# Quartered divisions in two self attentions, the last experts' answers as rows, and answers fetched in two parts

## The chip, the core and the metric

The kernel runs on one core of a Trainium2 chip. A core has a matrix engine (TensorE, "PE" in the profile, its weight loads "PEld"), a vector engine (VectorE, "DVE"), a scalar engine (ScalarE, "ACT"), a general engine (GpSimd, "POOL") and a queue engine (SyncE, "SP"), which only issues transfers here. They run side by side, each through its own list of instructions in order, and wait for one another by semaphores. The metric is the device time of one execution in microseconds (us); lower is better.

## What is computed

A two-layer perceiver with 512 latent rows of width 512, 16 heads of 32, and a context of 8192 rows. Each layer is a cross attention into the context, a self attention, and a mixture of eight experts of which every row takes two. Everything is float32.

```python
x = x + L0_xattn(layernorm(x), ctx, key_mask, ...)      # LayerNorm on the heads of q and k
x = x + L0_attn(layernorm(x), ...)                      # softmax over j >= i
x = x + L0_ffn(layernorm(x), router, W1, W2)            # 8 experts, hidden width 2048, SiLU
x = x + L1_xattn(layernorm(x), ctx, mask, ...)
x = x + L1_attn(layernorm(x), ...)                      # 64 neighbours of each row
x = x + L1_ffn(layernorm(x), Wg, W1, W2)                # 8 experts, hidden width 1024, relu squared

def L1_ffn(x, Wg, W1, W2):
    probs = softmax(x @ Wg)
    top_w, top_i = top_k(probs, 2)
    top_w = top_w / (sum(top_w) + 1e-8)
    combine = sum(one_hot(top_i, 8) * top_w[..., None], axis=1)
    h = square(relu(einsum('td,edh->teh', x, W1)))
    y = einsum('teh,ehd->ted', h, W2)
    return einsum('te,ted->td', combine, y)
```

Which rows go to which expert depends on the data. The inputs are drawn from a fixed seed.

## The kernel before

The whole program is unrolled, and a scheduler orders each engine's list: an instruction that is ready in its model goes ahead of one that is not, and ties go by program order. So the order of the trace is that of the program with some instructions moved forward into holes. In time the stages are: cross attention 0 (0 to 467 us), self attention 0 (to 626), experts 0 (to 925), cross attention 1 (to 1333), self attention 1 (to 1443), experts 1 (to 1658), end (to 1667.9).

**Cross attentions** (`attend_slots`). The context is reduced to 15 tiles of 128 keys. Heads go in four groups `g` of four. For each group and tile a step computes scores (L787), subtracts the maximum (L668), takes the exponential (L914), and multiplies with the values (L864); the maxima of later groups are taken in the same steps, so that the last group's steps have none. When a group's 15 steps are over, its closing work is put as "fillers" behind the next group's steps: the sum of the exponentials (L894) at step 2, the division in quarters (`divide`, L906) at steps 3 to 6, then a multiplication and a bias on POOL (L909, L911), and the product with the output matrix (`k.outputs`, L744) at steps 9 and 10, followed by additions to the residual `x` on DVE (L750).

**Self attentions.** `in_order` goes through a string written by hand: `q`, `k` projections, `M` maxima, `S` the three parts of finding the shift of a group, `W` exponentials and sums, `F` the end of a group, `O` the output product in two halves. `F` copies the sum `o` and the denominator `d` out of PSUM on ACT, then does one reciprocal of 128x512 on DVE (L711), one multiplication on DVE (L712) and, in layer 0, a bias on ACT (L715). `S` needs DVE as well: a reduction (L682), a split into three bf16 parts (L690, L693), and a copy of the shift (L703), for which the matmuls of L668 wait.

**Experts** (`ffn`). Experts are sorted by the number of rows that they got. Eight places `r` hold the experts of rank `RANKS[r]`; place `r` has room for `caps[r]` rows, so all sizes are fixed. Per place the hidden width goes in `n` pieces of 512 (4 in layer 0, 2 in layer 1): `hidden` (L1828) computes 16 products of 128x128 weights with `caps[r]` columns of tokens, an activation follows on ACT and DVE, and `back` (L1844) does 16 more products into the accumulator `y`. Weights come by 1 MB transfers on SP (L1719, L1724) into four buffers each; a buffer comes free when the piece four places before it is done. A finished place is copied from `y` into `answers` by ACT and DVE (L1853, L1855); blocks of 128 answers are transposed on PE (L1860), copied (L1862) and stored to memory by POOL (`store`, L1869). Each row then fetches its two answers by indirect transfers on POOL (L1914, eight of 128 rows), and DVE adds them, scaled by the gate, to `x` (L1922). The last places, from `split` on, do not go through memory: their answers are transposed and multiplied with a matrix of gates (`gb`, `gated`), with `x` added by a product with the identity (L1926, L1927). In layer 0 that is place 7, in layer 1 places 6 and 7 (`by_dma` is 7 and 6).

**When an expert got more rows than its place has room for**, the flag `irow[E]` is set and every engine enters `rest` (L1939) instead of jumping over it. There, for each place in turn, the count is loaded and compared with `caps[r]`; where it is larger, the rows that found no room are gathered, the expert's weights are loaded again, and the two products are done for them. The rooms are

```python
CAPS0 = (132, 160, 152, 148, 140, 124, 116, 112)
CAPS1 = (112, 256, 224, 192, 160, 96, 64, 48)
```

Counted with the reference on its inputs, the experts of layer 0 get 105, 127, 131, 120, 148, 109, 143 and 141 rows and those of layer 1 get 47, 234, 157, 211, 108, 185, 59 and 23. Put in the order of the places, layer 0 has 127, 148, 143, 141, 131, 120, 109, 105 and layer 1 has 108, 234, 211, 185, 157, 59, 47, 23.

At the end `store_x` writes `x` out by one transfer (L2059), and a second test (L2077) jumps over a general version of the kernel for longer contexts.

Of the kernel before, what the change touches and what calls it, by code (L numbers as in the profile page):

```python
# [20 lines left out]
P = 128  # L21
# [16 lines left out]
CAPS0 = (132, 160, 152, 148, 140, 124, 116, 112)  # L38
CAPS1 = (112, 256, 224, 192, 160, 96, 64, 48)
BAND = 64  # L40
# [17 lines left out]
def tile_perceiver(  # L58
# [595 lines left out]
    def in_quads(pool, psum, pacc, qT, wo, bv, late, splits=None):  # L654
# [4 lines left out]
        count = [0]  # L659
        k = SimpleNamespace(ones32=ones[:, 0:HD], most={}, shifts={}, sums={}, o={}, bufs={"s": 3, "m": 3})  # L660

# [62 lines left out]
        def finish(g, pieces=1):  # L724

            if pieces > 1:
                for i in range(pieces):
                    r = slice(i * S // pieces, (i + 1) * S // pieces)
                    finish_part(g, r, k.sums[g][0][:, r], k.sums[g][1][:, r])
                return  # L730
            k.o[g] = late().tile([P, S], F32, name="o", tag="o", bufs=2)
            nc.scalar.copy(k.o[g], k.sums[g][0])
            d = late().tile([P, S], F32, name="d", tag="d", bufs=1)
            nc.scalar.copy(d, k.sums[g][1])
            divided(g, slice(0, S), d, d)

# [14 lines left out]

        k.tile_s, k.subtract, k.shift_of = tile_s, subtract, shift_of
        k.begin, k.finish, k.finish_part, k.outputs = begin, finish, finish_part, outputs
        return k

    def in_order(order, steps, k):


        shifts = {}
        for step in order.split():  # L760
            name, *n = step[0], *[int(v) for v in step[1:].split(".")]
            if name == "S":
                g, i = n
                if i == 0:
                    shifts[g] = k.shift_of(g)
                shifts[g][i]()
            elif name == "O":
                k.outputs(n[0], range(2 * n[1], 2 * n[1] + 2))
            else:
                steps[name](*n)  # L770

    def attend_slots(pool, psum, pacc, kT, vN, qT, kbias, wo, bv, late, keys, settle, values, unit, more, early, aside, beside, extra):
# [143 lines left out]
        for at in range(NG * n):  # L916
# [32 lines left out]
            if i == n - 1 and g < NG - 1:  # L949
                fillers.extend((  # L950
                    (at + 3, lambda g=g: denominators(g, range(len(parts[g])), len(parts[g]))),
                    *((at + 4 + j, lambda g=g, j=j: divide(g, j)) for j in range(4)),
                    (at + 10, lambda g=g: k.outputs(g, (0, 1))),
                    (at + 11, lambda g=g: k.outputs(g, (2, 3))),
                ))
# [348 lines left out]
    def self_attention0(pool):  # L1304
        with ExitStack() as st:
# [121 lines left out]
            def tail(t):  # L1427
# [3 lines left out]
                "q0 k0 q1 M0.0 k1 M0.1 M0.2 M0.3 q2 S0.0 S0.1 M1.0 k2 M1.1 S0.2 W0.0 M1.2 W0.1 M1.3 "  # L1431
                "W0.2 S1.0 W0.3 F0 S1.1 q3 M2.0 O0.0 M2.1 S1.2 k3 O0.1 M2.2 W1.0 M2.3 W1.1 M3.0 W1.2 S2.0 M3.1 "
                "W1.3 F1 S2.1 M3.2 M3.3 S2.2 W2.0 S3.0 W2.1 S3.1 W2.2 O1.0 W2.3 F2 O1.1 S3.2 W3.0 O2.0 W3.1 "
                "O2.1 E3 W3.2 E2 T3 W3.3 E1 T2 E0 T1 T0",
                {"q": query, "k": key, "M": maxima, "W": weighted, "F": finish, "E": end, "T": tail}, k,
            )

    def self_attention1(pool):

        W = S + 2 * PAD  # L1440
        with ExitStack() as st:
# [71 lines left out]
            def finish(g):  # L1513
# [15 lines left out]
            in_order(  # L1529
                "q0 k0 M0 q1 S0.0 k1 S0.1 M1 q2 S0.2 S1.0 W0 k2 S1.1 M2 F0 S1.2 q3 S2.0 W1 k3 S2.1 "  # L1530
                "O0.0 M3 F1 S2.2 O0.1 S3.0 W2 S3.1 O1.0 F2 O1.1 S3.2 W3 O2.0 F3 O2.1 O3.0 O3.1",
                {"q": query, "k": key, "M": maxima, "W": weighted, "F": finish}, k,
# [177 lines left out]
    def ffn(wp, pool, w1, w2, ff, layer, act, softmax_first, caps, order):  # L1710
# [20 lines left out]
        with ExitStack() as st:  # L1731
# [23 lines left out]
            def get(i):  # L1755
                if i not in pieces and i < E * n:
                    pieces[i] = weights(experts[i // n], i % n)
                return pieces.get(i)

# [5 lines left out]
            accs = {}  # L1765

            by_dma = E - 1
            while total - starts[by_dma - 1] <= P:
                by_dma -= 1
            split = starts[by_dma]  # L1770
            tail = total - split

            def one_hot(to, r, gated):
# [26 lines left out]
            def transposed(b):  # L1800
# [15 lines left out]
                return go  # L1816

            def hidden(i):
                r, c = divmod(i, n)
                k = caps[r]  # L1820
                w1, _ = get(i)
                hT = inner.tile([P, NC, W], F32, name="hT", tag="hT", bufs=2)
                for h in range(2):
                    ps = psum.tile([P, 2, W], F32, name="hps", tag="h", bufs=4)
                    for j in range(2):
                        f = 2 * h + j
                        for c in range(NC):
                            nc.tensor.matmul(  # L1828
                                ps[:, j, 0:k], lhsT=w1[:, c, f * P : (f + 1) * P], rhs=tokens[:, c, starts[r] : starts[r] + k],
                                start=(c == 0), stop=(c == NC - 1),  # L1830
                            )
                    act(inner, hT[:, 2 * h : 2 * h + 2, 0:k], ps[:, :, 0:k])
                return hT

            def back(i, hT):
                r, c = divmod(i, n)
                k = caps[r]
# [26 lines left out]

            def store(b):

                m = min(P, split - b * P)
                rows = rows_of(answers, b * P, m, "yb")
                nc.gpsimd.dma_start(out=answers_d[1 + b * P : 1 + b * P + m, :], in_=rows[0:m, :])  # L1869

# [12 lines left out]
            for _ in range(3):  # L1883
                fetch()
            last, done, blk = None, 0, 0
            for i in range(E * n):
                hT = hidden(i)
                for j in range(1, 4):
                    get(i + j)
                if last is not None:  # L1890
                    back(i - 1, last)
                    if i % n == 0:
                        done = min(starts[i // n], split)
                    elif (blk + 1) * P <= done or (done == split and blk * P < done):
                        store(blk)
                        blk += 1
                last = hT
                r = i // n
                if i % n == n - 2 and r + 1 < E:
                    while waiting and waiting[0][0] * P < starts[r + 1] + caps[r + 1]:  # L1900
                        waiting.pop(0)[1]()
                        fetch()
                if i == 1:
                    of, gates = answers_of()
                    for q in range(by_dma, E):
                        one_hot(gated[:, :, starts[q] - split : starts[q] - split + caps[q]], q, True)
                if i == n * by_dma + 1:
                    while blk * P < split:
                        store(blk)
                        blk += 1  # L1910
                    for j in range(2):
                        for t in range(NT):
                            got = inner.tile([P, D], F32, name="got", tag="got", bufs=8)
                            nc.gpsimd.indirect_dma_start(  # L1914
                                out=got, out_offset=None, in_=answers_d,
                                in_offset=bass.IndirectOffsetOnAxis(ap=of[:, j * NT + t : j * NT + t + 1], axis=0),
                            )
                            late.append((got, gates[:, j, t : t + 1], t))
                    gb = rows_of(gated, 0, tail, "gb", 1)
            back(E * n - 1, last)  # L1920
            for got, g, t in late:
                nc.vector.scalar_tensor_tensor(x[:, t, :], got, g, x[:, t, :], ALU.mult, ALU.add)  # L1922
            yb = rows_of(answers, split, tail, "yb")
            for t in range(NT):
                ps = psum.tile([P, D], F32, name="xps", tag="h", bufs=4)
                nc.tensor.matmul(ps, lhsT=ident, rhs=x[:, t, :], start=True, stop=False)  # L1926
                nc.tensor.matmul(  # L1927
                    ps, lhsT=gb[0:tail, t * P : (t + 1) * P], rhs=yb[0:tail, :], start=False, stop=True
                )
                if layer == 0:  # L1930
                    x_from(t, ps)
                else:
                    (nc.scalar.copy if t % 2 else nc.vector.tensor_copy)(x[:, t, :], ps)

# [4 lines left out]
        with tc.If(flag > 0):  # L1939
            rest(wp, pool, weights, irow, place, gate, xn, n, act, caps)  # L1940
            for t, st in stats.items():
                nc.vector.bn_stats(st, x[:, t, :])
# [114 lines left out]

    def store_x():
        nc.sync.dma_start(out=out.rearrange("b (t p) d -> p (b t) d", p=P), in_=x)  # L2059

# [10 lines left out]
    rest_of_layer1()  # L2071
    store_x()
    n = nc.values_load(
# [3 lines left out]
    with tc.If(n > SLOTS):  # L2077
# [16 lines left out]
        rest_of_layer1()  # L2094
        store_x()

# [108 lines left out]
```

## Time and profile before

| | us |
|---|---|
| runs before, median of 3 | 1666.83 (1665.01 to 1671.99) |
| the profiled execution, its own time | 1669.63 |
| its span, first to last instruction | 1667.9 |
| PE busy | 1540.8 (92%) |
| PEld busy | 924.8 (55%) |
| DVE busy | 758.8 (45%) |
| ACT busy | 602.0 (36%) |
| POOL busy | 450.1 (27%) |

The profiled execution is 2.8 us above the median of the runs, and its time is 1.73 us above its span. A line of the timeline has the start, the length, the engine, the line of the program, the operation with the tiles that it writes and reads, the number of instructions, and in brackets how long the engine had been idle and for whom. "x8" on PE counts passes: a float32 product is two of them, so a product of a 128x128 weight tile with 512 columns is two passes, and 16 products are x32. PEclk is the share of the full clock that TensorE was granted.

### The profile page before, as it was taken

What the parts mean: (1) busy time and instruction counts of PE and PEld (TensorE: products, weight loads), DVE (VectorE), ACT (ScalarE), POOL (GpSimd) and SP (SyncE); (2) the same over time, 40 slices, a digit from 0 to 9 for tenths busy, and PEclk for the clock granted to TensorE, in tenths of its full rate; (3) what the DMA queues carried; (4) which work ended last, traced back from release to release, by engine and by line L of the source; (5) the groups of instructions that cost most, each with busy time, mean ns of one, the idle gap of its engine ahead of it and who ended that gap; (6) DMA issues with size and microseconds to landing.
All of it is one profiled execution on the core that took longest, in us unless ns stands there. A gap on an engine that the chain in (4) does not pass through costs nothing. (4 is left out here: it accounts for less than half of the span.)

```text
span 1667.9 us, 25506 instructions
## 1 busy us (share of the span) xinstructions
PE 1540.8 (92%) x10565; PEld 924.8 (55%) x10565; DVE 758.8 (45%) x1380; ACT 602.0 (36%) x1132; POOL 450.1 (27%) x350
## 2 busy tenths in 40 slices
PE   5898999999899996999999899999999899779996
PEld 2333344333244446999999465434333245479995
DVE  5366677874425553111112135577875418531101
ACT  2265465566532242111111311176567523301110
POOL 7000068877110011000002100077885210010001
PEclk9998999999999887999999899999999999779996
DMA  7154100000120005877886400000000310085662
GB/s 253 45 182 135 61 26 2 1 2 1 52 81 1 1 2 206 314 256 266 282 293 201 134 26 19 26 1 2 1 1 1 120 44 2 26 297 189 202 222 87
DMA packets 83935, 169.42 MB, mean 102 GB/s; under 512 B 5106, under 2 KB 20498, under 8 KB 82384
## 3 DMA queue, kind: packets, MB, share of 16 engines
q1 hardware_dynamic: 77200, 147.87, 26.1%
q0 software_dynamic: 6016, 17.55, 3.1%
q10 hardware_dynamic: 576, 2.10, 0.4%
q8 instruction: 89, 1.46, 0.4%
q14 instruction: 54, 0.44, 0.1%
HBM read 156.82 MB, written 9.63 MB: 100 GB/s over the span
## 5 line engine op out<-in xcount | busy, mean ns | idle before, releaser
L914 ACT ACTIVATE pT<-sc,kbias 128x512 f32<-128x512 f32 x480 | 297.9, 696 | 156.2 <-PE sc L668 141.5
L787 PE MATMUL sc<-qTf,kTf 32*128 32x512 f32 x1264 | 291.1, 647 | 8.7 <-ACT vNf L1064 4.6
L800 DVE SCALAR_TENSOR_TENSOR mx<-scm,kbias,mx 128x512 f32<-128x512 f32 x312 | 218.1, 741 | 72.6 <-PE scm L787 72.1
L1844 PE MATMUL y<-hT,w 128*128 128x112 f32 (+13 forms) x1536 | 211.1, 297 | 0.9 <-DVE hT L2025 0.9
L787 PE MATMUL scm<-qTf,kTf 32*128 32x512 f32 x656 | 211.3, 639 | 0.0
L1828 PE MATMUL hps<-tokens,w 128*128 128x112 f32 (+13 forms) x1536 | 206.7, 293 | 0.0
L1844 PEld LDWEIGHTS y<-hT,w 128*128 128x128 f32 x1536 | 204.4, 197 | 2.8 <-DVE hT L2025 1.1
L1828 PEld LDWEIGHTS hps<-tokens,w 128*128 128x128 f32 x1536 | 199.7, 193 | 1.6
L885 POOL TENSOR_TENSOR four<-four,pT 128x2048 f32<-128x2048 f32 x42 | 190.7, 4540 | 10.3 <-ACT pT L914 7.9
L787 PEld LDWEIGHTS sc<-qTf,kTf 32*128 32x128 f32 x1264 | 80.9, 185 | 128.4 <-issue 79.1
L864 PE MATMUL acc<-pT,vNf 128*32 128x256 f32 (+1 forms) x1600 | 144.8, 434 | 1.5 <-ACT o L874 1.5
L885 POOL TENSOR_TENSOR four<-pT 128x2048 f32<-128x2048 f32 x24 | 109.0, 4543 | 53.2 <-ACT pT L914 53.2
L800 DVE SCALAR_TENSOR_TENSOR mx<-sc,kbias,mx 128x512 f32<-128x512 f32 x136 | 93.4, 743 | 56.5 <-PE sc L787 56.5
L2025 DVE TENSOR_TENSOR hT<-sg,hps 128x264 f32<-128x264 f32 (+7 forms) x64 | 27.9, 436 | 191.0 <-ACT sg L2024 191.0
L864 PEld LDWEIGHTS acc<-pT,vNf 128*32 128x32 f32 x1600 | 32.1, 108 | 130.1 <-issue 124.3
L668 PE MATMUL sc<-shift,ones 3*128 3x512 bf16 (+3 forms) x544 | 91.9, 372 | 3.6 <-DVE shift L703 3.6
L1869 POOL DMA_DIRECT2D answers_d<-yb x17 | 9.4, 556 | 311.6 <-ACT yb L1862 311.5
L787 PEld LDWEIGHTS scm<-qTf,kTf 32*128 32x128 f32 x656 | 73.0, 183 | 3.6 <-DVE mx L800 1.8
L2024 ACT ACTIVATE sg<-hps 128x264 f32<-128x264 f32 (+7 forms) x64 | 25.3, 396 | 135.7 <-PE hps L1828 135.7
L1055 PE MATMUL pk<-wkvf,cslot 128*128 128x512 f32 x120 | 59.4, 641 | 5.4 <-DVE kb L1094 5.4
L2030 DVE TENSOR_TENSOR hT<-sg 128x224 f32<-128x224 f32 (+7 forms) x32 | 14.7, 458 | 107.1 <-ACT sg L2029 107.1
L682 DVE TENSOR_REDUCE neg<-mtp 128x4 f32<-128x512 f32 x64 | 41.2, 683 | 47.2 <-PE mtp L679 47.2
(358 smaller groups left out, 1897.2 us busy)
## 6 DMA issues: line engine op xcount, KB each, us to landing
w<-in_L_ffn_W SPq DMA_DIRECT2D x96, 1024.0 KB, 7.5
mi<-in_mask SPq DMA_DIRECT2D x32, 512.0 KB, 4.5
cslot<-in_ctxT SPq DMA_DIRECT2D x30, 256.0 KB, 5.0
answers_d<-yb POOLq DMA_DIRECT2D x15, 256.0 KB, 6.8
answers_d<-zero POOLq DMA_DIRECT2D x9, 256.0 KB, 6.7
wkvf<-in_L_xattn_WkvT ACTq DMA_DIRECT2D x4, 512.0 KB, 6.9
wq<-in_L_xattn_WqT SPq DMA_DIRECT2D x2, 1024.0 KB, 8.0
wof<-in_L_xattn_WoT SPq DMA_DIRECT2D x2, 1024.0 KB, 4.7
```

The lines of the kernel that those rows point to most:

```text
L668: nc.tensor.matmul(ps, lhsT=ones16[r, :], rhs=k.shifts[g][r, 0:w], start=start, stop=stop)
L682: nc.vector.tensor_reduce(neg[:, h, :], tp.rearrange("p (t k) -> p t k", k=P), AX.X, ALU.max, negate=True)
L787: nc.tensor.matmul(ps, lhsT=kT[HD * h : HD * (h + 1), g, i * P : (i + 1) * P], rhs=qT[HD * h : HD * (h + 1), g, :], start=True, stop=stop,)
L800: nc.vector.scalar_tensor_tensor(to, ps, b, to, ALU.add, ALU.max)
L864: nc.tensor.matmul(k.sums[g][HD * h : HD * (h + 1), r], lhsT=vN[:, i, g * P + HD * h : g * P + HD * (h + 1)], rhs=pT[:, h, r], start=(i == ...
L885: engine.tensor_tensor(to, parts[g][-1], pT, ALU.add)
L914: nc.scalar.activation(pT[:, h, :], ps, AF.Exp, bias=kbias[:, i : i + 1])
L1055: last = nc.tensor.matmul(ps.rearrange("p (g n) -> p g n", g=NG), lhsT=src[:, c, s % 2, :], rhs=wkv[:, :, c, i * P : (i + 1) * P], start=( ...
L1828: nc.tensor.matmul(ps[:, j, 0:k], lhsT=w1[:, c, f * P : (f + 1) * P], rhs=tokens[:, c, starts[r] : starts[r] + k], start=(c == 0), stop=(c ...
L1844: nc.tensor.matmul(accs[0][:, d, 0:k], lhsT=w2[:, f, d * P : (d + 1) * P], rhs=hT[:, f, 0:k], start=(c == 0 and f == 0 and d % 2 == 0), st ...
L2024: nc.scalar.activation(sg, ps, AF.Sigmoid)
L2025: nc.vector.tensor_tensor(dst, sg, ps, ALU.mult)
```

## The change

Six edits go together.

1. `CAPS1` becomes `(112, 256, 224, 192, 144, 96, 64, 64)`: place 4 has room for 144 instead of 160, place 7 for 64 instead of 48.
2. In `attend_slots` the output products of the last group but one (`NG - 2`) move from steps 9 and 10 of the next group to steps 12 and 13.
3. In the self attentions `F` only copies `o` and `d`. A new step `D` takes the reciprocal of a quarter; the fourth also multiplies, on POOL, and in layer 0 adds the bias on ACT. The strings are rewritten, with `O` later.
4. The last places' answers are computed as rows: the 512 columns of a weight piece are the moving operand, and the tokens or hidden values are the stationary one. In layer 1 places 6 and 7 (64 rows each) share the two halves of one tile, for `hidden` too, whose result is transposed by PE.
5. Stores go as soon as a block is complete, also right after a place's last piece; blocks end at the start of place `by_dma - 1`. The fetches are split: the first of a row's two answers by place order is fetched while piece `n * by_dma - 1` is worked on, the other one piece later. The additions stand before the last `back`.
6. In layer 1 the residual is added by DVE from PSUM instead of by a product with the identity, and `x` is stored in four transfers, once in `ffn` and once more at the end of `rest`.

```diff
-CAPS1 = (112, 256, 224, 192, 160, 96, 64, 48)
+CAPS1 = (112, 256, 224, 192, 144, 96, 64, 64)
...
-            d = late().tile([P, S], F32, name="d", tag="d", bufs=1)
-            nc.scalar.copy(d, k.sums[g][1])
-            divided(g, slice(0, S), d, d)
+            k.d[g] = late().tile([P, S], F32, name="d", tag="d", bufs=1)
+            nc.scalar.copy(k.d[g], k.sums[g][1])
+
+        def quarter(g, i):
+
+            r = slice(i * S // 4, (i + 1) * S // 4)
+            tc.keep_in_program_order(nc.vector.reciprocal(k.d[g][:, r], k.d[g][:, r]))
+            if i < 3:
+                return
+            nc.gpsimd.tensor_tensor(k.o[g], k.o[g], k.d[g], ALU.mult)
+            if bv is not None:
+
+                nc.scalar.activation(k.o[g], k.o[g], AF.Identity, bias=bv[:, g : g + 1])
...
-                    (at + 10, lambda g=g: k.outputs(g, (0, 1))),
-                    (at + 11, lambda g=g: k.outputs(g, (2, 3))),
+                    (at + (13 if g == NG - 2 else 10), lambda g=g: k.outputs(g, (0, 1))),
+                    (at + (14 if g == NG - 2 else 11), lambda g=g: k.outputs(g, (2, 3))),
...
-                "W0.2 S1.0 W0.3 F0 S1.1 q3 M2.0 O0.0 M2.1 S1.2 k3 O0.1 M2.2 W1.0 M2.3 W1.1 M3.0 W1.2 S2.0 M3.1 "
-                "W1.3 F1 S2.1 M3.2 M3.3 S2.2 W2.0 S3.0 W2.1 S3.1 W2.2 O1.0 W2.3 F2 O1.1 S3.2 W3.0 O2.0 W3.1 "
-                "O2.1 E3 W3.2 E2 T3 W3.3 E1 T2 E0 T1 T0",
+                "W0.2 S1.0 W0.3 F0 S1.1 q3 D0.0 D0.1 M2.0 D0.2 M2.1 D0.3 S1.2 k3 M2.2 W1.0 O0.0 M2.3 W1.1 O0.1 "
+                "M3.0 W1.2 S2.0 M3.1 W1.3 F1 S2.1 M3.2 D1.0 M3.3 S2.2 D1.1 W2.0 D1.2 S3.0 W2.1 D1.3 S3.1 W2.2 "
+                "O1.0 W2.3 F2 S3.2 D2.0 D2.1 O1.1 W3.0 D2.2 D2.3 W3.1 E3 O2.1 W3.2 O2.0 E2 T3 W3.3 E1 T2 E0 T1 T0",
...
-                "q0 k0 M0 q1 S0.0 k1 S0.1 M1 q2 S0.2 S1.0 W0 k2 S1.1 M2 F0 S1.2 q3 S2.0 W1 k3 S2.1 "
-                "O0.0 M3 F1 S2.2 O0.1 S3.0 W2 S3.1 O1.0 F2 O1.1 S3.2 W3 O2.0 F3 O2.1 O3.0 O3.1",
+                "q0 k0 M0 q1 S0.0 k1 S0.1 M1 q2 S0.2 S1.0 W0 k2 S1.1 M2 F0 S1.2 q3 D0.0 D0.1 S2.0 W1 D0.2 D0.3 "
+                "k3 S2.1 M3 F1 S2.2 O0.0 D1.0 D1.1 S3.0 O0.1 W2 D1.2 D1.3 S3.1 F2 O1.0 S3.2 D2.0 O1.1 W3 D2.1 "
+                "D2.2 D2.3 O2.0 F3 O2.1 O3.0 O3.1",
...
+            def hidden_rows(i):
+
+                ws = [get(j)[0] for j in order_of[i]]
+                ps = psum.tile([P, S], F32, name="hrow", tag="h", bufs=4)
+                for c in range(NC):
+                    for j, w in enumerate(ws):
+                        lo = split + j * P // 2
+                        nc.tensor.matmul(
+                            ps[j * P // 2 : (j + 1) * P // 2, :], lhsT=tokens[:, c, lo : lo + P // 2], rhs=w[:, c, :],
+                            start=(c == 0), stop=(c == NC - 1),
+                        )
+                rows = inner.tile([P, S], F32, name="hN", tag="hN", bufs=2)
+                act(inner, rows, ps)
...
+            def back_rows(i, hT):
...
+                for f in range(NC):
+                    for j, w in enumerate(ws):
+                        nc.tensor.matmul(
+                            y[j * m : (j + 1) * m, :], lhsT=hT[:, f, j * m : (j + 1) * m], rhs=w[:, f, :],
+                            start=(c == 0 and f == 0), stop=(c == n - 1 and f == NC - 1),
+                        )
...
+                to = inner.tile([P, S], F32, name="yb", tag="yb", bufs=2)
+                nc.scalar.copy(to[0:tail, :], y[0:tail, :])
...
+                    store(done)
...
+                if i == n * by_dma - 1:
+                    while store(done):
+                        pass
+                    fetch_answers(1)
+                if i == n * by_dma:
+                    while store(done):
+                        pass
+                    fetch_answers(0)
+                if i == units - 1:
                     gb = rows_of(gated, 0, tail, "gb", 1)
+                    add_answers()
+            yb = back(units - 1, last)
             for t in range(NT):
                 ps = psum.tile([P, D], F32, name="xps", tag="h", bufs=4)
-                nc.tensor.matmul(ps, lhsT=ident, rhs=x[:, t, :], start=True, stop=False)
+                if layer == 0:
+                    nc.tensor.matmul(ps, lhsT=ident, rhs=x[:, t, :], start=True, stop=False)
...
-                    (nc.scalar.copy if t % 2 else nc.vector.tensor_copy)(x[:, t, :], ps)
+                    nc.vector.tensor_tensor(x[:, t, :], x[:, t, :], ps, ALU.add)
+                    store_x(t)
...
             rest(wp, pool, weights, irow, place, gate, xn, n, act, caps)
+            if layer > 0:
+                for t in range(NT):
+                    store_x(t)
```

## The prediction

> **What bounds the kernel now.** I read the busy shares, then the slices with the clock, each engine's timeline around PE's holes, and the instructions of the two tests. PE is busy 92% of the span, so the time is PE's list plus its holes, and after a hole PE runs at half clock:
>
> ```profile
> PE   5898999999899996999999899999999899779996
> ...
> PEclk9998999999999887999999899999999999779996
> ```
>
> Each digit is a fortieth of the span (41.7 us). A hole at the end of cross attention 1, on PE and then on POOL:
>
> ```profile
> 1293.81 1.06 PE L864 MATMUL acc<-pT,vNf 128*32 128x512 f32 x8
> 1300.40 3.78 PE L744 MATMUL ops<-wof,o 128*128 128x512 f32 x4 [5.53 <-POOL o L911]
> ```
> ```profile
> 1296.82 3.52 POOL L911 TENSOR_SCALAR o<-o,L_xattn_bv 128x512 f32<-128x512 f32 x1
> ```
>
> PE's list has the output product where POOL's bias is not done. In the self attentions the undivided reciprocal stands on DVE ahead of what PE needs:
>
> ```profile
> 570.49 3.35 DVE L711 RECIPROCAL d<-d 128x512 f32<-128x512 f32 x1
> ```
> ```profile
> 574.44 0.79 PE L1353 MATMUL sc<-qTs,kTs 32*128 32x128 f32 x2 [2.71 <-DVE neg L682]
> ...
> 603.04 0.62 PE L668 MATMUL sc<-shift,ones 3*128 3x512 bf16 x4 [3.56 <-DVE shift L703]
> ...
> 1427.77 0.61 PE L668 MATMUL shf<-shift,ones 3*128 3x512 bf16 x4 [4.30 <-DVE shift L703]
> ```
>
> At the end of experts 1 the last place's 48 columns run at half clock, and POOL is still fetching:
>
> ```profile
> 1630.72 12.40 PE L1844 MATMUL y<-hT,w 128*128 128x48 f32 x64
> ...
> 1641.62 0.95 POOL L1914 DMA_INDIRECT got<-answers_d,rows_of  x1 [0.30 <-issue]
> ```
>
> And the jumps over `rest` and over the general version:
>
> ```profile
> L1939 PEldq COMPARE_BRANCH  x2: 3626/3742/3859, 918.8 to 1649.6; - x2
> ```
> ```profile
> L2077 ACTq EVENT_SEMAPHORE  x2: 17/17/17, 1666.2 to 1666.2; - x2
> ...
> L2077 ACTq COMPARE_BRANCH  x1: 50/50/50, 1661.1 to 1661.1; - x1
> ```
>
> PE's sequencer stands 3.7 us in a taken jump; ACT's next instruction comes 5.1 us after its own. From `x` complete (1657.65) to the end of the span take 10.25 us.
>
> **Part by part**, in us of this execution, each stage on its old clock.
>
> *Cross attentions, 15.7 saved.* The move is by three steps. A step takes 2.29 (1290.22 to 1292.50) on PE and 2.42 on ACT (four exponentials), so PE comes to the product at 1294.87 + 3 x 2.3 = 1301.8; `o` is ready at 1296.82 + 3.52 = 1300.34. The margin of 1.4 is the cover; without it the difference comes back as a wait. Gone are the hole of 5.53, the half clock of this product (3.78 against 1.98 for the next one) and of the scores behind it (1.38 against 1.14), and a wait of 0.29: 7.9. The same hole stands in cross attention 0 (5.52 at 432.64). Range 8 to 17.
>
> *Self attention 0, 9 saved.* Holes of 0.69, 2.71 and 3.56; half clock over 570 to 590 (clock 0.66, so up to 0.34 x 17.3 busy = 5.9) and in the product at 603.59 (3.78 against 1.98): at most 14.7. A quarter takes 0.95 (L906), so the shift's chain on DVE waits for one at most, but its reductions and splits remain, and `o` gains a way over POOL (1.28 to 3.12, L909) before ACT's bias; the affine selects (0.64) and the last `O2` queue behind that POOL multiplication. DVE itself gets 4 x 0.95 for 3.35 + 0.68. I take about 60%; bounds -3 (a new wait before `O2`) and 14.7.
>
> *Self attention 1, 5 saved.* Holes of 0.89, 1.51, 0.82, 0.23, 4.30, and 3.2 of half clock (0.60 over 1428 to 1436): 11 at most. But DVE is busy 9.97, 7.98 and 9.93 of the three tens from 1390 to 1420, and quarters take no work from it; only the order helps. Bounds 0 and 11.
>
> *Experts 0, 4 saved.* The last place's `back` costs the same: 4 products of 512 columns (8 passes of 0.43, as eight of L1204 in 3.43) for 16 (x32 in 3.55). At the end, the wait for `hT` behind DVE's additions (0.92) goes, and so does the chain copy, transpose, copy, transpose, copy from 914.68 to 918.17, but for one copy of 0.59: 3.8. One product of the residual more comes ahead: 5. Against it, a block is now stored right after its place's last piece, whose two copies take 0.8 (887.20 to 887.99); seven blocks here, five in layer 1. PE would wait 10 in all if the scheduler put the transposes there; it fills such places with the next `hidden` (the transposes of blocks before stand between passes of L1828), so I charge 1, with 0 and 10 as bounds.
>
> *Experts 1, 31.6 saved up to `x` complete.* Place 4: 32 passes of 160 columns take 4.35, of 144 by proportion 3.92; four times, 1.7. The last two places took from 1603.52 to 1643.14. Now per piece 8 products of 512 columns, alone 6.9, two side by side 3.43. No row has two halves of 64 columns of weights; the nearest is the denominator, four strips of 32:
>
> ```profile
> L894 PE MATMUL den<-four,ones 128*32 128x512 f32 x240 | 27.6, 592 | 0.0
> ```
>
> 240 passes in 27.6 are 0.115 each, against 0.43 alone: four at a time. I take two at a time; if not, each of four costs 3.43 more. In order: `hidden` 3.43, `back` of place 5 3.57, transposes 0.9, `hidden` 3.43, then twice transposes 0.44 and `back` 3.43, `gb` 0.45, and 1.5 of waits for activations: 21, so answers at 1603.5 - 1.7 + 21 = 1622.9. Then copy 0.59, four products 0.86 each with no identity, one addition 0.69: `x` at about 1626 instead of 1657.65. What could be late: the last weight transfer still waits for `back` of place 5 (about 1609), lands 7.5 later (median), and is wanted at 1619. POOL's last store goes at 1611, lands after 2.1 to 5.7, four fetches at 1.25 end by 1622, land 3.6 later: level with `x`, up to 3 more.
>
> On two half-blocks the Trainium skill speaks against me: "TensorE: Matmul & The Clock Gate", Part 3, The mechanism, says that a weight load passes a running product only where the row groups differ, and the halves use all rows. By it the stage would cost 13.7 more. The denominators' row has full row groups too and runs four at once, so the measurement decides.
>
> *`rest` runs in layer 1, and costs 46.* Place 4 got 157 rows and now has room for 144. So `irow[E]` is set, and `rest` opens place 4 for 13 rows (with 112 columns), jumping over the other seven. No run shows it; I build it up from 1626.
> - PE: each jump 3.73, the count's load 0.31 and two semaphore instructions, 4.3. The first is taken ahead of the matmuls, as at 1649.6, but behind each jump stands a wait for PE's own last matmul (1657.2); three remain: 13, so PE opens the expert at 1639.
> - SP: four stores must land first (5.5 as `out_x`), then 4 loads and jumps (0.5 to 3), so weights are asked for at about 1637 and the first is there at 1642 (least landing 4.9).
> - The expert: gather, two `hidden`, two `back`, each x32 at 3.55, 17.8; half clock after the hole, 5; activations, copies, transposes 3; four products and an addition 4.1: done at about 1669, at once stored again.
> - PE jumps three places and the general version, the first ahead: 13, then 1.7 as now: end at 1683.
>
> That is 57 behind `x` for 10.25, or 46 more. Bounds: 30 (near jumps cost nothing, PE waits for weights alone) and 95 (rival 1). By "Runtime: NRT & Kernel Launch", Instruction fetch mechanics, a jump stalls only where its target is outside the window already fetched. By that the small bodies on DVE, ACT and SP could be jumped for nearly nothing, and the sum would come near its lower bound; no row here has a near jump.
>
> **Sum:** -15.7 - 9 - 5 - 4 - 31.6 + 46 = -19.3 on a span of 1667.9, so 1648.6; with 1.7 around it, 1650.3. The profiled run lies 2.8 above the median, so I predict 1648.
>
> **Rivals.**
> 1. *`rest` costs more than all savings.* Place: the eight jumps. If each costs every engine ACT's 5.1 (41), and the expert runs at half clock throughout (2 x 17.8 + 9 = 45), the end is 1626 + 41 + 45 + 10 = 1722; minus 33.7 saved in earlier stages and plus 1.7 - 2.8, 1687: slower. It decides once `rest` and the end take over 75 instead of my 57. For: nothing in it overlaps. Against: PE's jumps show 3.7, and half clock never lasted over 15 us while PE was kept fed.
> 2. *The half-blocks do not run side by side:* 4 x 3.43 = 13.7 more, 1662, no change. For: the rule above; against: the denominators.
> 3. *`rest` is not entered,* so the change does only what it says: 10.25 behind 1626, 1601. For: no row of this profile shows `rest`. Against: 157 is counted from the reference, whose top two the kernel takes as well.
>
> **How the numbers follow.** The forecast 0.66, with its own range 1630 to 1664 (self attentions 0 to 20 saved, `rest` 35 to 60); rival 1 0.15, rival 2 0.12, rival 3 0.07. Beyond 0.5% (8.3 us) a measurement of this kernel tells a change: faster is under 1658.5, slower above 1675.2. Faster: 0.85 of the forecast, half of rival 2, rival 3: 0.68. Slower: rival 1 and a tail: 0.17. The rest is 0.15. The range 1620 to 1682 leaves out rival 3 and most of rival 1.
>
> **What would show it.** No hole before L744 in either cross attention; DVE's 0.95 quarters and no 3 us wait for L703; a dense PE to about 35 us before the old end of experts 1, with a full clock; then new lines (gather, `hidden`, `back` of `rest`) on 112 columns after seven short jumps. Wrong would be: no lines of `rest`, passes of the half-blocks at 0.43 apiece, or `rest` over 75.

## The result, and the profile after

| | before | after |
|---|---|---|
| median of 20 runs each, us | 1669.28 (1661.55 to 1679.19) | 1669.68 (1666.31 to 1678.27) |
| the profiled execution, its own time | 1669.63 | 1667.95 |
| its span | 1667.9 | 1666.2 |
| PE busy | 1540.8 | 1533.6 |
| mean granted clock | 0.947 | 0.957 |

The ratio is 1.002 (95% interval 1.0004 to 1.0037; that of the two medians alone is 1.0002): no change by the bound of the prediction, which expected 1648 and a clear gain. The time lies inside the range of 1620 to 1682.

The change does move time, in both directions. In the table, stages begin where PE transposes the normalised rows (`lnt`); from one such place to the next the two profiled executions take, in us:

| stage | before | after | difference | predicted |
|---|---|---|---|---|
| cross attention 0 and 1 | 443.3 + 404.7 | 434.6 + 397.8 | -15.6 | -15.7 |
| self attention 0 | 157.5 | 151.3 | -6.2 | -9 |
| experts 0 | 305.2 | 302.0 | -3.2 | -4 |
| self attention 1 | 110.5 | 106.5 | -4.0 | -5 |
| experts 1, up to `x` complete | 211.7 | 191.9 | -19.8 | -31.6 |
| from `x` complete to the end | 10.25 | 57.2 | +47.0 | +46 |

`x` is complete at 1657.65 before and at 1608.96 after; experts 1 begin at 1446.0 and 1417.1. The slices of the page of after:

```profile
PE   5898999999999987999998999999999998699955
...
PEclk9999999999999988999999999999999999699988
```

The slice with clock 0.6 (1416 to 1458) is the start of experts 1, which was there before as well. The last two slices, from 1583 on, are half empty at a clock of 0.8: there the time is lost that the earlier stages gained.

The timeline of PE in cross attention 1, where the product of the last group but one now stands:

```profile
1284.14 1.06 PE L877 MATMUL acc<-pT,vNf 128*32 128x512 f32 x8
1285.14 1.99 PE L755 MATMUL ops<-wof,o 128*128 128x512 f32 x4
1287.05 1.14 PE L800 MATMUL sc<-qTf,kTf 32*128 32x512 f32 x8
```

and POOL's bias ahead of it:

```profile
1280.23 3.50 POOL L924 TENSOR_SCALAR o<-o,L_xattn_bv 128x512 f32<-128x512 f32 x1
```

No idle time in brackets, 1.99 for the product instead of 3.78, 1.14 for the scores instead of 1.38. POOL ends at 1283.73, so 1.4 of margin are left.

DVE and PE in self attention 0. The quarters lie between the steps of the shift's chain, and the hole of 3.56 before L668 is gone; a smaller one stands elsewhere:

```profile
563.71 0.94 DVE L740 RECIPROCAL d<-d 128x128 f32<-128x128 f32 x1
...
565.30 0.42 DVE L703 COPY shift<-stp 128x512 bf16<-128x512 bf16 x1
565.64 1.75 DVE L740 RECIPROCAL d<-d 128x128 f32<-128x128 f32 x2
```
```profile
589.64 0.66 PE L1433 MATMUL accq<-pT,vNs 128*32 128x128 f32 x8 [2.22 <-POOL pT L1410]
```
```profile
587.73 1.26 POOL L743 TENSOR_TENSOR o<-o,d 128x512 f32<-128x512 f32 x1 [6.52 <-DVE d L740]
588.95 0.64 POOL L1410 TENSOR_SCALAR_AFFINE_SELECT pT<-pT 128x512 f32<-128x512 f32 x1
```

The affine select for which PE waits is queued behind POOL's new multiplication: the stall has moved from DVE to POOL. In self attention 1 PE's list has two holes over 1 us, 1.93 (1399.92, `<-ACT pTw L1524`, an exponential) and 1.43 (1405.27, `<-POOL o L743`), for the 4.30 of before; only the second is POOL's.

Experts 1, the two half-blocks, on PE:

```profile
1575.27 3.65 PE L1846 MATMUL hrow<-w,tokens 128*64 128x512 f32 x16
...
1582.60 1.07 PE L1846 MATMUL hrow<-w,tokens 128*64 128x512 f32 x2
...
1588.23 0.42 PE L1931 MATMUL stp<-ident,answers 128*96 128x128 f32 x2 [4.21 <-DVE answers L1926]
...
1588.70 5.34 PE L1846 MATMUL hrow<-w,tokens 128*64 128x512 f32 x14
```

16 passes in 3.65 are two at a time. But the second set is broken by a hole of 4.21, after which its 14 passes take 5.34, at a lower clock (0.71 granted over 1588.2 to 1594.0, 1.00 over the first set). PE waits for a copy on DVE, and DVE's list says why that is late:

```profile
1587.16 0.75 DVE L1962 SCALAR_TENSOR_TENSOR x<-got,gates,x 128x512 f32<-128x512 f32 x1 [6.86 <-DMA got<-answers_d,rows_of]
1587.83 0.35 DVE L1926 COPY answers<-y 128x192 f32<-128x192 f32 x1
```

The addition of the first fetched answers stands ahead of the copy. The fetch's landing ends the wait, although the copy's own input was there at 1582.7.

Then `rest`. PE's holes, and the jumps (duration least/median/greatest in ns, first and last start):

```profile
1621.83 6.07 PE L2062 MATMUL gps<-at,xn 128*128 128x112 f32 x32 [13.61 <-DVE at L2057]
1627.74 3.74 PE L2076 MATMUL hps<-xg,w 128*128 128x112 f32 x32
...
1631.31 3.98 PE L2083 MATMUL y<-hT,w 128*128 128x112 f32 x32
```
```profile
1621.08 0.84 DVE L2057 TENSOR_SCALAR at<-steps,off 128x112 f32<-128x112 f32 x4 [7.70 <-PEq L2048]
```
```profile
L2048 ACTq COMPARE_BRANCH  x9: 38/45/50, 1604.7 to 1645.9; - x9
L2048 PEldq COMPARE_BRANCH  x9: 70/2733/5542, 1605.5 to 1656.1; - x9
L2048 DVEq COMPARE_BRANCH  x9: 50/56/69, 1609.4 to 1650.9; - x9
```

112 columns are the lines of `rest` for place 4. On DVE, ACT and SP the branch of a place's test takes about 0.05. On PE it is long, though not everywhere: of the seven places that it jumps over, two take 0.42 and 0.44 and the other five 2.7 to 5.5. DVE is held by that: it waits 7.70 for PE's sequencer, which is still jumping.

### The profile page after: what moved, and what is told of

Same layout as the page of the kernel before. It is cut to its first block, busy times and chain, and to the rows that moved or that the text cites. A ratio compares the mean times of both kernels' runs of the same rounds, so it can differ in the third digit from the quotient of the medians.

```text
span 1666.2 us, 25489 instructions
## 1 busy us (share of the span) xinstructions
PE 1533.6 (92%) x10445; PEld 898.7 (54%) x10445; DVE 764.6 (46%) x1406; ACT 605.1 (36%) x1141; POOL 458.0 (27%) x356
## 5 line engine op out<-in xcount | busy, mean ns | idle before, releaser
L1897 PE MATMUL hps<-tokens,w 128*128 128x112 f32 (+12 forms) x1408 | 193.2, 294 | 0.0
L1897 PEld LDWEIGHTS hps<-tokens,w 128*128 128x128 f32 x1408 | 184.6, 192 | 2.7 <-issue 1.0
L1915 PE MATMUL y<-hT,w 128*128 128x132 f32 (+12 forms) x1280 | 176.1, 296 | 0.9 <-DVE hT L2117 0.9
L1915 PEld LDWEIGHTS y<-hT,w 128*128 128x128 f32 x1280 | 170.0, 193 | 3.5 <-DVE hT L2117 1.1
L2117 DVE TENSOR_TENSOR hT<-sg,hps 128x264 f32<-128x264 f32 (+7 forms) x64 | 27.8, 436 | 174.3 <-ACT sg L2116 174.3
L668 PE MATMUL sc<-shift,ones 3*128 3x512 bf16 (+3 forms) x544 | 93.4, 373 | 0.0
L1068 PE MATMUL pv<-wkvf,cslot 128*128 128x512 f32 x120 | 60.2, 645 | 0.0
```

The source lines that it names most:

```text
L668: nc.tensor.matmul(ps, lhsT=ones16[r, :], rhs=k.shifts[g][r, 0:w], start=start, stop=stop)
L1068: last = nc.tensor.matmul(ps.rearrange("p (g n) -> p g n", g=NG), lhsT=src[:, c, s % 2, :], rhs=wkv[:, :, c, i * P : (i + 1) * P], start=( ...
L1897: nc.tensor.matmul(ps[:, j, 0:k], lhsT=w1[:, c, f * P : (f + 1) * P], rhs=tokens[:, c, starts[r] : starts[r] + k], start=(c == 0), stop=(c ...
L1915: nc.tensor.matmul(accs[0][:, d, 0:k], lhsT=w2[:, f, d * P : (d + 1) * P], rhs=hT[:, f, 0:k], start=(c == 0 and f == 0 and d % 2 == 0), st ...
L2117: nc.vector.tensor_tensor(dst, sg, ps, ALU.mult)
```

## The experiments

Ratios are to the kernel before, run beside each on the same chip, with the 95% interval.

**Rooms that fit.** Is it `rest` that takes the gain?

```diff
-CAPS1 = (112, 256, 224, 192, 144, 96, 64, 64)
+CAPS1 = (112, 240, 224, 192, 160, 96, 64, 64)
```

> The changed kernel with rooms that fit: place 1 has 240 instead of 256, place 4 has 160 instead of 144, the sum is again 1152. Theory A (what the change saves is real, and `rest` gives it back): no lines of `rest`; `x` complete at 1609 as in the changed kernel (1608.96), the end 10 behind it instead of 57.2, so 47 less: about 1621, ratio to the kernel before 0.972. Rival B (`rest` is mostly hidden, or the end would be waiting for the stores and the sequencers anyway): 1650 or more, ratio over 0.988.

Measured: 0.9738 (0.9716 to 0.9761), median 1620.94. No line of `rest` in the trace; `x` complete at 1607.67 and the span's end at 1618.2, 10.5 later. Theory A holds, to 1 us; B falls.

**`rest` alone.** The same from the other side, on the kernel before:

```diff
-CAPS1 = (112, 256, 224, 192, 160, 96, 64, 48)
+CAPS1 = (112, 256, 224, 192, 144, 112, 64, 48)
```

> The kernel before with place 4 at 144 instead of 160 and place 5 at 112 instead of 96, so that `rest` is entered for 13 rows and nothing else changes. Theory A: from `x` complete to the end 57 instead of 10.25, 47 more: 1713 to 1718, ratio 1.028. Of it 13 until PE opens the expert, 28 for the expert, 16 to the end. Rival B (`rest` costs far less by itself, and something else of the change is slow): under 1695, ratio under 1.016.

Measured: 1.0293 (1.0272 to 1.0314), median 1715.71. `x` is complete at 1650.51, the span ends at 1709.8: 59.3 instead of 10.25, 49 more. PE opens the expert 14 behind `x`, and its last addition ends at 1692.45, 28 later; 17.3 remain to the end. A holds.

**What in `rest` costs it.** The rooms that fit, but layer 1 enters `rest` where no place has too many rows, so that it only tests and jumps:

```diff
-        with tc.If(flag > 0):
+        with tc.If((flag > 0) if layer == 0 else (flag < 1)):
```

> The rooms that fit, but in layer 1 `rest` is entered where the flag is 0, so all eight places are tested and jumped and no expert is done. Theory A (the jumps and their waits make about half of `rest`): 13 until PE has jumped four places as in the changed kernel, 4.5 for the fifth, 11 for the other three, 6 for the general version: 35 behind `x` instead of 10.25, so 1645 against 1621 with the rooms that fit, ratio 0.988. Rival D (nearly all of the 47 is the expert itself; near jumps are cheap on every engine): 1621 to 1627, ratio under 0.977.

Measured: 0.9863 (0.9824 to 0.9903), median 1648.36. The instructions of the tests in this trace:

```profile
L2048 ACTq COMPARE_BRANCH  x8: 45/45/50, 1602.2 to 1606.9; - x8
...
L2048 PEldq COMPARE_BRANCH  x8: 2700/3368/5362, 1603.0 to 1634.4; - x8
...
L2048 DVEq COMPARE_BRANCH  x8: 56/56/63, 1606.9 to 1614.5; - x8
```

ACT tests all eight places in 5 us, DVE in 8, PE in 34. From `x` complete (1606.47) to the end (1644.0) take 37.5, against 10.5 without `rest`: 27 come from tests and jumps with no expert at all, and they are PE's alone, since the last jump of any other engine ends before 1619 and PE's at 1642.1. A holds, D falls. In the changed kernel the split is somewhat different, since two of PE's jumps are short there: its seven jumps add up to 20.2, the eight here to 29.6. The stretch of the expert is 27.8 there, and what lies before and behind it is 19.2 more than the 10.25 of before. So of the 47 between 19 and 27 are tests and jumps.

**Additions behind the copy.** The eight additions of fetched answers are kept in program order, in the changed kernel and in the one with rooms that fit (lines behind it are two higher):

```diff
-                    nc.vector.scalar_tensor_tensor(x[:, t, :], got, g, x[:, t, :], ALU.mult, ALU.add)
+                    tc.keep_in_program_order(
+                        nc.vector.scalar_tensor_tensor(x[:, t, :], got, g, x[:, t, :], ALU.mult, ALU.add)
+                    )
```

> The changed kernel with the eight additions of fetched answers pinned behind what stands ahead of them on DVE. Theory A (the hole of 4.21 in experts 1 comes from an addition that waits for its fetch ahead of the copy that the last store needs): the copy stands at about 1583, no hole before the transposes, the second pair of half-blocks takes 3.65 instead of 1.07 + 5.34; `x` complete 6 earlier at 1603, time 1662, ratio 0.9965 to the kernel before. Rival C (the store or the fetch is late for another reason, POOL or the landing): PE waits elsewhere for as long, `x` at 1607 to 1610, ratio 1.000 to 1.003.

> Both edits: rooms that fit, and additions behind the copy. If A holds for both, the two gains add up: 47 + 6 less than the changed kernel, 1615, ratio 0.968. If the hole only hid another wait (C): 1620, as with the rooms alone.

Measured: 0.9955 (0.9939 to 0.9972), median 1659.25, and 0.9675 (0.9658 to 0.9692), median 1612.76. DVE and PE of the first:

```profile
1582.59 0.36 DVE L1926 COPY answers<-y 128x192 f32<-128x192 f32 x1 [2.76 <-ACT answers L1924]
...
1597.27 0.75 DVE L1963 SCALAR_TENSOR_TENSOR x<-got,gates,x 128x512 f32<-128x512 f32 x1 [5.80 <-DMA got<-answers_d,rows_of]
...
1602.01 2.48 DVE L2023 TENSOR_TENSOR x<-x,xps 128x512 f32<-128x512 f32 x4
```
```profile
1583.13 0.64 PE L1931 MATMUL stp<-ident,answers 128*96 128x128 f32 x4
...
1583.82 3.65 PE L1846 MATMUL hrow<-w,tokens 128*64 128x512 f32 x14
```

The copy follows its input at once, the hole is gone and the passes run at full clock (1.00 granted). From the first half-block pass to the first product of `gb`, PE takes 23.14 instead of 29.26. Theory A holds, C falls. `x` itself comes only 4.5 earlier in its stage, since the last fetched answers now end last: their additions run to 1602.0, and only then the four additions of `xps`. The two gains add up: 1612.76 is 8.2 below the rooms alone.

**One fetch.** With rooms that fit and additions in order, is the split of the fetch worth anything?

```diff
-                if i == n * by_dma - 1:
-                    while store(done):
-                        pass
-                    fetch_answers(1)
...
+                    fetch_answers(1)
                     fetch_answers(0)
```

> Rooms that fit and additions behind the copy, with both fetches again behind the last store instead of half of them ahead of it. Theory G (the split holds the last store back: POOL stands 3.72 until the first fetches have landed before it may write the answers again): the store goes at about 1579.6 instead of 1585.98, eight fetches of 1.27 follow its landing from 1582.6, the last at 1591.5 instead of 1592.41, so `x` 0 to 2 earlier than with the split; time 1611 to 1613, ratio 0.966 to 0.968. Rival H (the split hides four fetches, as its place suggests): they follow one another behind the store and the end comes 4 to 5 later, ratio 0.970 or more.

> Rooms that fit and additions behind the copy once more, beside the last one on the same chip: 1612 to 1615, ratio 0.966 to 0.969, so that a difference of 2 us to it can be read.

Measured: 0.9667 (0.9635 to 0.9698) with one fetch, 0.9656 (0.9628 to 0.9685) with two; the intervals overlap. POOL with two, in the trace of the first run with rooms that fit and ordered additions:

```profile
1581.31 0.95 POOL L1953 DMA_INDIRECT got<-answers_d,rows_of  x1 [0.30 <-issue]
1585.98 0.58 POOL L1946 DMA_DIRECT2D answers_d<-yb  x1 [3.72 <-DMA got<-answers_d,rows_of]
1588.64 0.97 POOL L1953 DMA_INDIRECT got<-answers_d,rows_of  x1 [2.08 <-DMA answers_d<-yb]
```

and POOL with one, where the store's rows (ready at 1579.4 with two, at 1579.1 with one) go at once:

```profile
1579.42 0.55 POOL L1946 DMA_DIRECT2D answers_d<-yb  x1 [8.38 <-ACT yb L1933]
1583.62 1.01 POOL L1953 DMA_INDIRECT got<-answers_d,rows_of  x1 [3.65 <-DMA answers_d<-yb]
...
1593.07 0.95 POOL L1953 DMA_INDIRECT got<-answers_d,rows_of  x1 [0.30 <-issue]
```

With the split, the last store waits 3.72 for the landing of the first four fetches, which read the memory that it writes to; what they hide is given back there. From the first half-block pass to `x` complete it is 31.1 and 31.4 with two fetches (two runs) and 31.6 with one. H falls; G's wait is there, and the landing of the store (3.65 instead of 2.08) and the issues (up to 1.5 apart) ate the 1 us that it should have left.

**The half-blocks in turn.** The rooms that fit, with the loops turned round, in `hidden_rows` and `back_rows`:

```diff
-                for c in range(NC):
-                    for j, w in enumerate(ws):
+                for j, w in enumerate(ws):
+                    for c in range(NC):
```

> The rooms that fit, with the loops over the two half-blocks turned round: all products of the first 64 rows, then all of the second. Theory A (two half-blocks run side by side because successive passes go to different halves of the tile): 16 passes take 7.0 instead of 3.65, four times, 13.5 more than with the rooms alone: 1634, ratio 0.982. Rival E (the order makes no difference: a pass of 64 columns of weights takes 0.23 whatever stands beside it): 1621, ratio 0.974.

Measured: 0.9712 (0.9667 to 0.9758), which overlaps the rooms alone. The time can't decide, since the hole before L1931 shrank from 5.61 to 1.85 in this trace and took most of the difference. The passes can:

```profile
1593.56 5.42 PE L1875 MATMUL y<-w,hT 128*64 128x512 f32 x16 [0.24 <-ACT hT L1858]
```

5.42 for 16 passes, neither 7.0 (A) nor 3.65 (E). Single records show why: the first four passes of one half start 0.43 apart; from the fifth on, passes of the other half start in the same 0.43, four pairs, and its last four are alone again: 12 steps of 0.43 with the ends. So two halves do run side by side, and the other half's first pass starts while three passes that stand ahead of it in PE's list have not begun, but no earlier; the three groups of 16 that no hole breaks all take 5.42. Why it starts there is not shown. The order in the change, with the halves alternating, is what gets 3.65.

**The attentions alone,** each on the kernel before: the cross attentions' move (edit 2), and the self attentions' quarters (edit 3).

> The kernel before with the output products of the last group but one three steps later, and nothing else. Theory A: the two cross attentions are 8.65 and 6.8 shorter, as in the changed kernel, 15.5 in all: ratio 0.9907. Rival F (part of it is a faster clock that the whole changed kernel has, or is given back in the next stage): under 10, ratio over 0.994.

> The kernel before with the quartered divisions and the new orders of the two self attentions, and nothing else. Theory A: 6.2 and 3.9 less, as in the changed kernel: ratio 0.994. Rival F (part of it is given back in the experts, whose first weights and clock do not move with it): under 5, ratio over 0.997.

Measured: 0.9877 (0.9841 to 0.9913) and 0.9910 (0.9876 to 0.9943), 20.6 and 15 by the middle of the interval. Both hold the expected ratio, near their upper ends, and neither is F's. The stages are a finer measure: over this and the other runs, with the old code (before, `rest` alone and the other of these two) the cross attentions take 440.9 and 403.4 on average, with the new one (nine profiles) 433.2 and 395.6: 15.5. Self attention 0 goes from 157.1 to 151.7, and 1 from 110.4 to 106.4: 9.4 in all. One cross attention scatters by 7 us between executions of the same code (430.0 to 437.0), more than any single hole here.

## Why the prediction was wrong

The direction was missed, by one step above all. Put beside the runs:

- *Cross attentions, 15.7:* right, 15.6 in the profile and 15.5 over all profiles, and for the reason given: the margin was worked out as 1.4 and is 1.4.
- *Self attentions, 9 and 5:* right in kind, a little too much; 6.2 and 4.0. The bound named "a new wait before `O2`" by the way over POOL; two such waits are there (2.22 and 1.43), the first of them for an affine select that had to queue behind POOL's multiplication. A third (1.93) is for ACT.
- *Experts 0, 4:* 3.2, and 1.5 on average over all profiles, which scatter by 4.7 there. No run has the edits to the experts alone.
- *Experts 1, "31.6 saved up to `x` complete":* **this is the step that failed**; 19.8 came. Of the 11.8 missing, 6.1 are the hole behind DVE's addition with the lower clock after it, as the run with ordered additions shows on PE (29.26 against 23.14; `x` gets back 4.5 of it, since the fetched answers then end last). The prediction watched when the fetches would land, but not what stands behind the waiting additions on DVE: the scheduler placed the first one ahead of the copy which the last store needs. Another 1.5 are longer passes (3.65 and 3.81 for 3.43 and 3.57) and waits for activations above the 1.5 allowed. 2.4 are a later start of the first half-block, 158.2 into the stage instead of 155.8. The 1.7 for narrower columns in place 4 is there: a group of 32 passes takes 4.09 (at 1541.19), before 4.51 (at 1568.76), and there are four. But 32 transposes of answers (L1931) stand ahead of this point instead of 16 (L1860), since stores now go as soon as a block is complete, and the stretch is 0.8 longer in spite of the 1.7: about 2.5 for four blocks. The prediction charged the earlier stores 1 in experts 0 and nothing here. And 1.6 is a slip of addition: 1622.9 with the copy, four products and the last addition is 1627.6, not 1626. The few tenths that remain are in the last four products.
- *`rest`, 46:* right in sum, 47.0, and in its parts: PE opens the expert 12.9 behind `x` (13 predicted), the expert takes 27.8 to its last addition (30), 16.6 remain to the end (14). Alone it costs 49. That the 13 fits is partly luck: it was worked out as three more jumps of 4.3 each, and in the trace the branches of the three take 0.42, 4.63 and 5.54. The prediction's own terms give 57 less 10.25, which is 46.75 and not 46. The page "Runtime: NRT & Kernel Launch" of the Trainium skill, Instruction fetch mechanics, has a taken branch stall where its target lies outside the window already fetched. The jumps over the short bodies on DVE, ACT and SP fit that (0.05 each), though no run shows which targets lie in the window. But the conclusion that the sum then comes near its lower bound does not follow: five of PE's seven jumps over a place still take 2.7 to 5.5, and DVE waits for PE.
- *The median:* 2.8 was taken off because the profiled run lay that far above three runs. With 20 runs before's median is 1669.28, and the 2.8 was chance.

So the sum missed by 17.7 on the profiled execution (1667.95 against 1650.3): 11.8 in experts 1, 4.8 in the earlier stages, 1 in `rest`. The other 4 of the 21.7 between 1648 and 1669.68 are the correction to the median (2.3) and the profiled run of after, which lies 1.7 under its own. Every saving came in below what was taken for it, that of the cross attentions by 0.1 only, and with 65 of savings against 46 of cost a loss of a quarter of the savings leaves nothing. (The chances given for "faster" add up to 0.69, not 0.68.)

*The rivals.* 1 falls in its mechanism: ACT tests and jumps all eight places in 5 us, not in 5.1 each, and `rest` and the end took 57.2, far from its 75. 2 falls: 3.65 for 16 passes. The rule weighed against the change, that a weight load passes a running product only where row groups differ ("TensorE: Matmul & The Clock Gate" of the Trainium skill, Part 3, The mechanism), does not hold for halves of columns: these passes use all rows and still run in pairs, as the denominators' row suggested. 3 is excluded by the lines of `rest`, but the rooms that fit show its case: 1620.94, not 1601, by the same misses. Its condition is the gain that the change gives away.

A version that beats both kernels is the changed one with rooms (112, 240, 224, 192, 160, 96, 64, 64) and ordered additions: 1612.76 and 1612.96, ratios 0.9675 and 0.9656.

## What to carry to other kernels

Where sizes are fixed and the data decides, look first at whether the data fits: one room of 144 for 157 rows cost 47 us, nearly all that the other edits had saved (48.7), and moving 16 rows of room from a place with 22 to spare got it back. When transfers are fetched earlier, ask what stands behind their consumers: an instruction that waits for a transfer belongs behind what others wait for on its engine. And where many small savings stand against one large cost, give each saving its own likely loss.

## What was not expected of the hardware

- The same test and jump over a place costs engines very differently: eight of them took ACT 5 us, DVE 8 and PE 34, with branches of 0.045, 0.056 and 2.7 to 5.4 each. What PE jumps over is far longer than what the others do (176 passes with their loads for place 4 in the changed kernel's trace, 21 instructions on DVE); that the length is the reason is not shown, and in the changed kernel two of PE's seven jumps took only 0.4.
- PE starts a pass of 64 columns of weights beside one for the other half even when three passes of the first half that stand ahead of it in the list have not begun: passes do not start strictly in the order of the list. With eight of one half ahead of eight of the other the first four ran alone: 16 passes took 3.65 alternating and 5.42 in turn.
- A store to memory that earlier indirect fetches read from waited 3.5 to 3.9 for their landing on POOL (three runs with ordered additions), so fetching half early moved no time that can be told from the scatter.
